# Keys of an attention layer from seven products of halves, laid between the value products, with a gate tensor reloaded per batch

## The chip, the cores and the metric

The kernel runs on one core of a Trainium2 chip. The metric is the device time in microseconds (us) of one execution. Engines are named as in the profile: PE (TensorE: matmul; PEld is its weight load), DVE (VectorE), ACT (ScalarE), POOL (GpSimd), SP (SyncE, which issues the DMAs here). All data are f32.

## The reference, cut to what matters

There are 16 batches of N = 1024 nodes with C = 256 channels. Layer 0 is attention with 4 heads of 64, whose queries come from a gate on an adjacency matrix; layer 1 is a two-stage graph convolution. Each ends in a residual and a layer norm. The part that the change touches:

```python
fea = jnp.transpose(x, (0, 2, 1))
A_s = ...                                  # likeness of the nodes, from channel means
Wg = adj[None, :, :] * A_s
g = jnp.einsum('bcn,bnm->bcm', fea, Wg)
g = jax.nn.relu(g * para.reshape(1, C, N)) # para: the gate tensor
q = jnp.transpose(g, (0, 2, 1)).reshape(B, N, h, hd).transpose(0, 2, 1, 3)
kv = (x @ kv_w).reshape(B, N, 2, h, hd).transpose(2, 0, 3, 1, 4)
k, v = (kv[0], kv[1])                      # keys and values: two halves of one product
attn = jax.nn.softmax(jnp.einsum('bhnd,bhmd->bhnm', q, k) * scale, axis=-1)
out = jnp.einsum('bhnm,bhmd->bhnd', attn, v)
```

The keys of one batch are thus a product of a 256 x 256 half of `kv_w` with the 256 x 1024 transposed input.

## The kernel before, in words

**Order.** Everything is written under a manual schedule: the order in which the program is written is the order of the instructions on each engine. Tiles come from pools; a new tile takes a free slot, and where none is free its first writer waits for the last reader of the old one. The row pool has 23 slots of one 128 x 1024 f32 tile (4 KB in each partition), `row_tile`. PSUM has three tiles of two banks (`big_psum`, or its first bank alone, `half_psum`) and two of one bank (`bank_psum`).

**The loop.** `run` (L834) goes over the batches. For batch b it does attention in four units (`UNITS`: two pairs of heads by two halves of the query nodes). `scores` (L506) computes eight score tiles; ACT takes each one's exponential (L517), and DVE adds them up into `acc` (L521, L523), transposes the sum (L525) and reduces it to `den_part` (L527). `outputs` (L529) multiplies the exponentials with the values and transposes the result on DVE (L538). `add` (L540) folds `den_part` into denominators by a small product on PE (L546), which DVE inverts (L550) and applies.

Between the units lie three gaps (`gap0`, `gap1`, `gap2`) with the graph convolutions of the two batches before: `inner` (L627), `Joined.run` (L796) and `last`. POOL prepares sums for them, `R` (L783 to L786) and, for the queries, `S` (L426 to L429). In `Joined.run` DVE adds a snapshot (L812), which ACT's `relu` (L645) reads; the result is transposed by DVE (L661).

**Queries.** The queries of batch b + 1 come from `FastQueries` (L404): instead of eight products of half matrices it does seven, on sums and differences of the halves, as in Winograd's form of Strassen's method. Its `end` (L469) combines the seven results on DVE (L477 to L484). `scale` (L487) multiplies with `para_sb`, which is on chip from the start, on DVE (L490) and applies a relu on ACT (L491).

**The batch change.** From batch 2's preparation on, the branch `elif more` (L1007 and on) has this order: the last query products, `q.end`, the DMAs for later batches (`load_blocked`, `load_next`), `keys` (L336), `norm.scale` (L325), `norm.spread` (transposes L213, stores L333), `values` (L349). `keys` makes two 128 x 1024 results from eight products of 128 x 128 with 128 x 512 and copies each on ACT (L346). Ahead of the last quarter it calls `between`: `norm.variance`, which folds squares on PE (L244), scales them on DVE (L318) and takes the power -1/2 on POOL (L320), and then `q.scale`. `values` makes four groups of two 128 x 256 blocks, each group in a one-bank PSUM tile, copied by ACT (L358). Then attention of batch b + 1 begins, and it reads `qT`, `kT` and `v`.

**SP's queue.** All loads and stores are issued there, in order. `Queries.load` (L371) issues the adjacency rows of the queries, `load_blocked` (L108) and `load_x` (L96) the inputs.

Of the kernel before, what the change touches and what calls it, by code (L numbers as in the profile page):

```python
# [18 lines left out]
def kernel(  # L19
# [31 lines left out]
    nc = tc.nc  # L51
# [14 lines left out]

    DEN_MIN = 1e-25
    DEN_MAX = 1e28
    ROWS = 23
    S = 32  # L70
    NB = N // S

# [18 lines left out]
    def bank_psum(name):  # L91
        return psum.tile([P, FB], F32, tag="bank", name=name, bufs=2)
# [6 lines left out]
    def row_tile(name):  # L99
        return work.tile([P, N], F32, tag="row", name=name, bufs=ROWS)  # L100

# [16 lines left out]
                          in_=x[0, t0 * P:(t0 + 2) * P, :].rearrange("(t p) c -> p t c", p=P))  # L118
    kvw_sb = const.tile([P, NC, 2 * C], F32, name="kvw_sb")
    nc.scalar.dma_start(out=kvw_sb, in_=kv_w.rearrange("(cc p) f -> p cc f", p=P))  # L120
    para_sb = const.tile([P, NC, N], F32, name="para_sb")
    w1l_sb = const.tile([P, NC, HID], F32, name="w1l_sb")
    w1n_sb = const.tile([P, NC, HID], F32, name="w1n_sb")
    w2l_sb = const.tile([HID, C], F32, name="w2l_sb")
# [1 line left out]
    b1_sb = const.tile([HID, 1], F32, name="b1_sb")  # L126
    b2_sb = const.tile([P, C], F32, name="b2_sb")

    def load_para():
        nc.sync.dma_start(out=para_sb, in_=para.rearrange("o (cc p) a b -> p (o cc) (a b)", p=P))  # L130

    def load_weights():
        nc.sync.dma_start(out=w1l_sb, in_=w1_loop.rearrange("(cc p) f -> p cc f", p=P))
# [67 lines left out]
    def adj_blocked(mt):  # L201
        t = row_tile(f"adjB_{mt}")
        for a in range(Q):
            nc.sync.dma_start(
                out=t[a * S:(a + 1) * S, :].rearrange("k (bn r) -> k bn r", r=S),
                in_=adj[:, mt * P + a * S:mt * P + (a + 1) * S].rearrange("(bn k) r -> k bn r", k=S))
        return t
# [84 lines left out]
    class BlockedNorm:  # L292


        def __init__(self, xB, sums, name):
            self.xB, self.sums, self.name = xB, sums, name
# [39 lines left out]
    def keys(b, xT, between=lambda: None):  # L336
        kT = work.tile([P, NC, N], F32, tag="kT", name=f"kT_{b}")
        for kb in range(NC):
            pk = big_psum(f"k_ps_{b}_{kb}")
            for j in range(NJ):  # L340
                if kb == 1 and j == 1:
                    between()
                for cc in range(NC):
                    nc.tensor.matmul(pk[:, ts(j, FB)], kvw_sb[:, cc, ts(kb, P)], xT[:, cc, ts(j, FB)],  # L344
                                     start=(cc == 0), stop=(cc == NC - 1))
            nc.scalar.copy(kT[:, kb, :], pk)  # L346
        return kT

    def values(b, xT, copy=nc.scalar.copy):  # L349
        v = work.tile([P, NT, C], F32, tag="v", name=f"v_{b}")  # L350
        per = FB // C
        for g in range(NT // per):
            pv = bank_psum(f"v_ps_{b}_{g}")
            for i in range(per):
                for cc in range(NC):
                    nc.tensor.matmul(pv[:, ts(i, C)], xT[:, cc, ts(g * per + i, P)], kvw_sb[:, cc, C:2 * C],  # L356
                                     start=(cc == 0), stop=(cc == NC - 1))
            copy(v[:, g * per:(g + 1) * per, :], pv.rearrange("p (i c) -> p i c", c=C))  # L358
        return v

    class Queries:

# [6 lines left out]
        def load(self, t):  # L369
            self.adj[t] = row_tile(f"adj_{self.b}_{t}")  # L370
            nc.sync.dma_start(out=self.adj[t], in_=adj[t * P:(t + 1) * P, :])  # L371

        def weigh(self, t):

# [22 lines left out]
        def end(self):  # L397
            qT = work.tile([P, NC, N], F32, tag="qT", name=f"qT_{self.b}")
            for cb in range(NC):
                nc.vector.tensor_mul(qT[:, cb, :], self.pg[cb], para_sb[:, cb, :])  # L400
                nc.scalar.activation(qT[:, cb, :], qT[:, cb, :], AF.Relu, scale=QSCALE)  # L401
            return qT

    class FastQueries(Queries):  # L404
# [82 lines left out]

        def scale(self):
            for cb in range(NC):
                nc.vector.tensor_mul(self.qT[:, cb, :], self.qT[:, cb, :], para_sb[:, cb, :])  # L490
                nc.scalar.activation(self.qT[:, cb, :], self.qT[:, cb, :], AF.Relu, scale=QSCALE)  # L491

    class Attention:
# [340 lines left out]
    def run():  # L834
# [11 lines left out]
        q = Queries(0, x_first)  # L846
        for t in range(NT):
            q.load(t)
        load_para()
        blocked = load_blocked(1, "1")  # L850
        tiles = {mt: adj_blocked(mt) for mt in range(3)}
        load_weights()
# [36 lines left out]
        for b in range(B):  # L889
# [57 lines left out]
                q = (FastQueries if c1 else Queries)(b + 1, xb)  # L947
            for u in range(len(UNITS)):
                att.scores(u)
                if u == 3 and between:  # L950
                    for t in (2, TJ + 2, 3, TJ + 3):
                        q.load(t)
                    for t in (2, TJ + 2, 3, TJ + 3):
                        q.likeness(t)
                    q.right(1)
                if u and not between:
                    att.add(u - 1)
                att.outputs(u)
                if u == 2 and more:
                    if c1:  # L960
                        for t in (1, TJ + 1):
                            q.load(t)
                            q.likeness(t)
                            q.times_adj(t)
                    else:
                        for t in range(3):
                            q.load(t)
                            q.weigh(t)
                if u < 3 and between:
                    between[u]()  # L970
                if u == 0 and more and not between:
                    means(q, xb, str(b + 1))()
            norm = BlockedNorm(xB, att.sums, str(b))
            if more and not c1:
                xT = ready["xT"]
                for t in range(3, NT):
                    q.load(t)
                for t in range(3, NT):
                    q.likeness(t)
                tiles[3] = adj_blocked(3)  # L980
                q.times_adj(3)
                q.step(0)
                q.times_adj(4)
                q.step(1)
                att.add(3)
                for mt in range(4, NT):
                    tiles[mt] = adj_blocked(mt)
                q.times_adj(5)
                q.step(2)
                q.step(3)  # L990
                norm.mean()
                q.times_adj(6)
                q.times_adj(7)
                q.step(4)
                norm.squares()
                norm.sum_squares()
                q.step(5)
                q.step(6)
                norm.variance()
                xB = load_blocked(b + 1, f"a{b + 1}")  # L1000
                q.step(7)
                qT = q.end()
                load_next()
                norm.scale()
                norm.spread()
                turn_adj(range(3, NT))
                kT, v = keys(b + 1, xT), values(b + 1, xT)  # L1007
            elif more:
                xT = ready["xT"]
                q.pair(2)  # L1010
                q.step(0)
                q.step(1, lambda: att.add(3))
                q.pair(3)
                q.step(2, lambda: (norm.mean(), norm.squares()))
                q.step(3)
                qT = q.end(norm.sum_squares)
                xB = load_blocked(b + 1, f"a{b + 1}")
                load_next()
                kT = keys(b + 1, xT, lambda: (norm.variance(), q.scale()))
                if not c2:  # L1020
                    adj_sums(rows01, 1)
                norm.scale()
                norm.spread()
                v = values(b + 1, xT)
            else:
                c2.load_h1()
                c2.load_x()
                both.fetch(2, 3)
                c1.inner()
                both.left(nc.gpsimd)  # L1030
                both.fetch(1, 4)
                both.run({1: (lambda: att.add(3),), 2: (norm.mean, norm.squares, norm.sum_squares), 7: (norm.variance,),
                          5: (norm.scale, norm.spread)})
                c1.turn(0)
                c2.last()
                c1.turn(1)
# [33 lines left out]
    with tc.If(count < P):  # L1070
        with tc.For_i(0, B, 1) as b:
            xb = load_x(b, "z")
            xT = channel_major(load_blocked(b, "z"), "xT_z")
            q = Queries("z", xb)
            means(q, xb, "z")()
            kT, v = keys("z", xT), values("z", xT)
            for t in range(NT):
                q.load(t)
                q.weigh(t)
                q.step(t)  # L1080
            safe_attention("z", xb, q.end(), kT, v)
            layernorm(xb, "za")
            conv = GraphConv("z", channel_major(blocked_of(xb, "z"), "x1T_z"), x=xb)
            rows01 = fetch("01", "z")
            conv.inner()
            conv.first(rows01)
            for j in range(NJ):
                conv.turn(j)
            conv.second(rows01)
            conv.last()  # L1090
            conv.moments()
            conv.finish(out[b])
# [29 lines left out]
```

## Time and profile before

Three runs took 2187.68, 2187.73 and 2188.1 us. The profiled execution took 2187.24 us, with a span of 2185.5 us on the core and a granted clock of 0.999.

| engine | busy us | share of the span | instructions |
|---|---|---|---|
| PE | 2168.6 | 99% | 8082 |
| DVE | 1801.7 | 82% | 2347 |
| ACT | 1016.2 | 46% | 1304 |
| POOL | 350.8 | 16% | 192 |

Busy time is the time in which an engine has at least one instruction at work. A row of the groups reads: line, engine, operation, output <- inputs with sizes in partitions x elements, count, then busy time and mean ns of one, then the engine's idle time ahead of them and what ended it. A row of the timeline gives start, length, engine, line, operation, and the count of instructions it joins; an idle time and its releaser stand in brackets. A row of the waits gives who waited for whom, the sum in us, the number of waits and the longest. The batch period in the middle of the run is 134.4 us (first key product at 657.74 us, the next batch's at 792.13 us).

### The profile page before, as it was taken

Reading aid. Unit: us, or ns where it says so; the run is one execution under the profiler, and the core shown is the slowest. Engines: PE = TensorE matmul, PEld = TensorE weight load, DVE = VectorE, ACT = ScalarE, POOL = GpSimd, SP = SyncE. Lnnn points to the kernel's source line nnn. Section 1 sums busy time; section 2 is a strip of 40 time slices with the busy share of each in tenths; the row PEclk is TensorE's granted clock in tenths of the full one; section 3 lists DMA queues with packets and bytes.
Section 4 is the critical chain, followed back from the end, with each engine's and each line's share of the span. In section 5 each row is a group of like instructions: output and inputs, shape, how many; then the busy total and the mean of one; then the engine's idle time right before and its main releaser. Section 6 shows DMA issues by size and latency. Waiting matters only on the chain.

```text
span 2185.5 us, 22862 instructions
## 1 busy us (share of the span) xinstructions
PE 2168.6 (99%) x8082; PEld 1029.9 (47%) x8082; DVE 1801.7 (82%) x2347; ACT 1016.2 (46%) x1304; POOL 350.8 (16%) x192
## 2 busy tenths in 40 slices
PE   9999999999999999999999999999999999999997
PEld 5344444444444444444544445444454444444354
DVE  4978978788898888978889788888888888888965
ACT  4744445544354544445443454444543445534411
POOL 0010120311303112030120302203022130211021
PEclk9999999999999999999999999999999999999999
DMA  9393653736547365563655526556374553743342
GB/s 223 92 121 116 140 149 86 144 118 98 154 107 152 101 94 156 107 161 87 91 170 97 155 87 91 169 97 155 87 105 155 99 153 96 123 138 61 113 138 95
DMA packets 604121, 266.54 MB, mean 122 GB/s; under 512 B 503904, under 2 KB 568288, under 8 KB 604000
## 3 DMA queue, kind: packets, MB, share of 16 engines
q1 hardware_dynamic: 603728, 264.49, 52.7%
q8 instruction: 65, 1.06, 0.2%
q10 hardware_dynamic: 272, 0.52, 0.1%
q14 instruction: 56, 0.46, 0.1%
HBM read 218.76 MB, written 46.20 MB: 121 GB/s over the span
## 4 chain that ended last, share of the span: by engine, by line
PE 69%; DVE 24%; ACT 4%; issue 2%; DMA 0%; DVEq 0%; SPq 0%; POOLq 0%; ACTq 0%; POOL 0%
PE s L514 17%; PE hu_ps L793 17%; PE av L534 16%; DVE acc L523 4%; PE v_ps L356 3%; PE t_ps L632 3%; PE h_ps L700 2%; PE hu_ps L639 2%; PE g_ps L394 2%; PE h_ps L701 2%; DVE wg L386 2%; DVE qT L490 1%; DVE sq_part L313 1%; ACT sq L308 1%; DVE wg L440 1%
## 5 line engine op out<-in xcount | busy, mean ns | idle before, releaser
L517 ACT ACTIVATE pr<-s 128x1024 f32<-128x1024 f32 x512 | 476.1, 1052 | 176.2 <-PE s L514 176.2
L523 DVE TENSOR_TENSOR acc<-acc,pr 128x1024 f32<-128x1024 f32 x384 | 493.4, 1285 | 41.4 <-DVE acc L523 1.4
L514 PE MATMUL s<-qT,kT 64*128 64x512 f32 x2048 | 457.1, 596 | 0.7 <-ACT qT L401 0.7
L534 PE MATMUL av<-pr,v 128*64 128x512 f32 x2048 | 453.6, 595 | 0.0
L514 PEld LDWEIGHTS s<-qT,kT 64*128 64x128 f32 x2048 | 191.2, 186 | 235.9 <-ACT pr L517 112.9
L534 PEld LDWEIGHTS av<-pr,v 128*64 128x64 f32 x2048 | 141.4, 137 | 300.0 <-issue 284.7
L320 POOL TENSOR_TENSOR rstd<-rstd,neg_half 128x32 f32<-128x32 f32 x16 | 100.2, 6260 | 1110.7 <-DVE rstd L318 1110.7
L380 ACT ACTIVATE wg<-c_row,c_col 128x1024 f32<-128x1024 f32 x128 | 147.0, 1149 | 74.2 <-DVE accB L525 55.7
L386 DVE SCALAR_TENSOR_TENSOR wg<-wg,adj 128x1024 f32<-128x1024 f32 x128 | 151.0, 1211 | 22.9 <-ACT wg L381 22.9
L793 PE MATMUL hu_ps<-adj,R 128*128 128x512 f32 x360 | 158.3, 596 | 0.0
L381 ACT ACTIVATE wg<-wg 128x1024 f32<-128x1024 f32 x128 | 135.4, 1058 | 4.1
L308 ACT ACTIVATE sq<-xB_a 128x1024 f32<-128x1024 f32 x32 | 33.8, 1057 | 188.7 <-DVE xB_a L303 187.4
L356 PE MATMUL v_ps<-kvw_sb,xT 128*128 128x256 f32 x512 | 117.0, 382 | 1.5 <-ACT v L358 0.8
L467 PE MATMUL g_ps<-wg,S 128*128 128x512 f32 x224 | 116.7, 603 | 0.0
L344 PE MATMUL k_ps<-xT,kvw_sb 128*128 128x512 f32 x256 | 115.8, 597 | 0.0
L467 PE MATMUL g_ps<-T,S 128*128 128x512 f32 x224 | 114.4, 592 | 0.0
L467 PE MATMUL g_ps<-wg,x 128*128 128x512 f32 x224 | 109.0, 599 | 0.0
L356 PEld LDWEIGHTS v_ps<-kvw_sb,xT 128*128 128x128 f32 x512 | 96.0, 190 | 26.7 <-issue 7.7
L793 PE MATMUL hu_ps<-adjT,t 128*128 128x512 f32 x240 | 105.7, 592 | 0.0
L793 PEld LDWEIGHTS hu_ps<-adj,R 128*128 128x128 f32 x360 | 67.3, 190 | 78.9 <-issue 78.7
L521 DVE TENSOR_TENSOR acc<-pr,pr 128x1024 f32<-128x1024 f32 x64 | 77.5, 1212 | 32.5 <-ACT pr L517 32.4
L325 DVE TENSOR_TENSOR xB_a<-xB_a,rstd 128x1024 f32<-128x1024 f32 x32 | 38.8, 1254 | 60.5 <-POOL rstd L320 60.5
(163 smaller groups left out, 2735.0 us busy)
## 6 DMA issues: line engine op xcount, KB each, us to landing
adj<-in_adj_dram SPq DMA_DIRECT2D x128, 512.0 KB, 4.5
adj<-adjT SPq DMA_DIRECT2D x120, 512.0 KB, 10.2
xB_a<-in_x_dram SPq DMA_DIRECT2D x128, 128.0 KB, 4.0
x1d<-xB_a SPq DMA_DIRECT2D x128, 128.0 KB, 3.4
x<-x1d SPq DMA_DIRECT2D x16, 1024.0 KB, 15.3
xB<-in_x_dram SPq DMA_DIRECT2D x120, 128.0 KB, 4.6
x<-in_x_dram SPq DMA_DIRECT2D x15, 1024.0 KB, 6.8
out_dram<-x SPq DMA_DIRECT2D x15, 1024.0 KB, 4.5
```

The lines of the kernel that those rows point to most:

```text
L320: nc.gpsimd.tensor_tensor(self.rstd, self.rstd, neg_half, ALU.pow)
L344: nc.tensor.matmul(pk[:, ts(j, FB)], kvw_sb[:, cc, ts(kb, P)], xT[:, cc, ts(j, FB)], start=(cc == 0), stop=(cc == NC - 1))
L356: nc.tensor.matmul(pv[:, ts(i, C)], xT[:, cc, ts(g * per + i, P)], kvw_sb[:, cc, C:2 * C], start=(cc == 0), stop=(cc == NC - 1))
L380: nc.scalar.activation(wg, self.c_row, AF.Abs, bias=self.c_col[:, t:t + 1], scale=-1.0)
L381: nc.scalar.activation(wg, wg, AF.Tanh, scale=-0.5)
L386: nc.vector.scalar_tensor_tensor(wg, wg, 1.0, self.adj.pop(t), op0=ALU.add, op1=ALU.mult)
L467: nc.tensor.matmul(self.p[n], x_n[:, k, :], w_n, start=(k == 0), stop=(k == TJ - 1))
L514: nc.tensor.matmul(ps[:, ts(s, FB)], self.kT[rows, pair, ts(mt, P)], self.qT[rows, pair, ts(j, FB)], start=True, stop=True)
L517: nc.scalar.activation(pr, ps, AF.Exp)
L523: nc.vector.tensor_add(acc, acc, pr)
L534: nc.tensor.matmul(pav[s * HD:(s + 1) * HD, :], self.v[:, mt, pair * P + s * HD:pair * P + (s + 1) * HD], self.pr[mt][:, ts(s, FB)], start ...
L793: nc.tensor.matmul(dst, self.x[n][:, k, :], half_adj[w][:, k, :] if w else of_rows(rows, k), start=(start and k == 0), stop=(k == TJ - 1), ...
```

## The change

The keys of batches 2 to 15 come from a new class `KeysValues`; batches 0 and 1 keep `keys` and `values`. `keys` itself is not changed, and `values` is split so that one group can be issued alone (`value_group`).

- The key product is divided into halves: the weights into four blocks of 128 x 128, the input into four of 128 x 512. Seven products of sums and differences replace the eight. The sums of weights are made once, at the start, by POOL, stored to DRAM and loaded per batch (`load`). The sums of the input halves are made per batch by DVE (`sums`), in unit 1 between `scores` and `outputs`.
- `run` issues the seven products with the four value groups between them. Five half results are copied on ACT, two sums are made on DVE and one on POOL. Three products accumulate on results that have been copied in between (`again=True`).
- `norm.variance` and `q.scale` are called at two places of that order, where `keys` called both at one.
- `para_sb` is no longer kept. Each batch loads its two rows (`load_para`), and the row pool has 25 slots in place of 23.

```diff
-    ROWS = 23
+    ROWS = 25
...
-    para_sb = const.tile([P, NC, N], F32, name="para_sb")
...
+    def sum_key_weights():
+        a11, a21, a12, a22 = (kvw_sb[:, cc, ts(kb, P)] for cc in range(NC) for kb in range(NC))
+        t = row_tile("key_sums")
+        s1, s2, s3, s4 = (t[:, ts(n, P)] for n in range(4))
+        nc.gpsimd.tensor_add(s1, a21, a22)
+        nc.gpsimd.tensor_sub(s2, s1, a11)
+        nc.gpsimd.tensor_sub(s3, a11, a21)
+        nc.gpsimd.tensor_sub(s4, a12, s2)
+        nc.sync.dma_start(out=key_sums, in_=t[:, 0:4 * P])
...
+    class KeysValues:
...
+        def sums(self):
+            w11, w12, w21, w22 = (self.xT[:, cc, ts(j, FB)] for cc in range(NC) for j in range(NJ))
+            t13, t24 = (row_tile(f"K_{self.b}_{k}") for k in range(2))
+            t1, t3, t2, t4 = t13[:, 0:FB], t13[:, FB:N], t24[:, 0:FB], t24[:, FB:N]
+            nc.vector.tensor_sub(t1, w12, w11)
+            nc.vector.tensor_sub(t3, w22, w12)
+            nc.vector.tensor_sub(t2, w22, t1)
+            nc.vector.tensor_sub(t4, w21, t2)
+            self.w = {1: w11, 2: w21, 3: w22, 4: t4, 5: t1, 6: t2, 7: t3}
+
+        def load(self):
+            t = row_tile(f"key_sums_{self.b}")
+            nc.sync.dma_start(out=t[:, 0:4 * P], in_=key_sums)
+            a11, a21, a12, a22 = (kvw_sb[:, cc, ts(kb, P)] for cc in range(NC) for kb in range(NC))
+            self.a = {1: a11, 2: a12, 3: t[:, ts(3, P)], 4: a22, 5: t[:, ts(0, P)], 6: t[:, ts(1, P)], 7: t[:, ts(2, P)]}
+
+        def run(self, between, later):
...
+            product(1, first)
+            nc.scalar.copy(p1, first)
+            product(2, third)
+            group(0)
+            product(6, first, again=True)
+            nc.scalar.copy(u1, first)
+            group(1)
+            between()
+            nc.vector.tensor_add(kT[:, 0, 0:FB], p1, third)
+            product(5, first, again=True)
+            nc.scalar.copy(u3, first)
+            product(7, second)
+            nc.scalar.copy(p7, second)
+            group(2)
+            later()
+            product(4, second, again=True)
+            nc.vector.tensor_add(kT[:, 1, 0:FB], u1, second)
+            nc.gpsimd.tensor_add(kT[:, 1, FB:N], u3, p7)
+            product(3, first, again=True)
+            nc.scalar.copy(kT[:, 0, FB:N], first)
+            group(3)
+            return kT, v
...
+        def load_para(self):
+            self.para = []
+            for cb in range(NC):
+                self.para.append(row_tile(f"para_{self.b}_{cb}"))
+                nc.sync.dma_start(out=self.para[cb],
+                                  in_=para[:, cb * P:(cb + 1) * P].rearrange("o p a b -> (o p) (a b)"))
...
         def scale(self):
             for cb in range(NC):
-                nc.vector.tensor_mul(self.qT[:, cb, :], self.qT[:, cb, :], para_sb[:, cb, :])
+                nc.vector.tensor_mul(self.qT[:, cb, :], self.qT[:, cb, :], self.para[cb])
...
-        load_para()
+        sum_key_weights()
+        q.load_para()
...
                 att.scores(u)
+                if u == 1 and between:
+                    kv = KeysValues(b + 1, ready["xT"])
+                    kv.sums()
...
                 q.step(2, lambda: (norm.mean(), norm.squares()))
+                q.load_para()
+                kv.load()
                 q.step(3)
                 qT = q.end(norm.sum_squares)
                 xB = load_blocked(b + 1, f"a{b + 1}")
                 load_next()
-                kT = keys(b + 1, xT, lambda: (norm.variance(), q.scale()))
+                kT, v = kv.run(norm.variance, q.scale)
                 if not c2:
                     adj_sums(rows01, 1)
                 norm.scale()
                 norm.spread()
-                v = values(b + 1, xT)
```

In the changed kernel's `run` the first three PSUM tiles are named `first`, `third` and `second`; `p1`, `u1`, `u3` and `p7` are halves of two row tiles in SBUF.

More of the change, by code (lines that the diff above doesn't have):

```diff
@@ L127 @@
     b2_sb = const.tile([P, C], F32, name="b2_sb")
-    def load_para():
-        nc.sync.dma_start(out=para_sb, in_=para.rearrange("o (cc p) a b -> p (o cc) (a b)", p=P))
+    key_sums = dram.tile([P, 4 * P], F32, tag="key_sums", name="key_sums", bufs=1)
+    def sum_key_weights():
[7 more added lines that the diff above has]
+        nc.sync.dma_start(out=key_sums, in_=t[:, 0:4 * P])
     def load_weights():
@@ L347, in keys, with value_group @@
         return kT
+    def value_group(b, v, xT, g, copy):
+        per = FB // C
+        pv = bank_psum(f"v_ps_{b}_{g}")
+        for i in range(per):
+            for cc in range(NC):
+                nc.tensor.matmul(pv[:, ts(i, C)], xT[:, cc, ts(g * per + i, P)], kvw_sb[:, cc, C:2 * C],
+                                 start=(cc == 0), stop=(cc == NC - 1))
+        copy(v[:, g * per:(g + 1) * per, :], pv.rearrange("p (i c) -> p i c", c=C))
     def values(b, xT, copy=nc.scalar.copy):
         v = work.tile([P, NT, C], F32, tag="v", name=f"v_{b}")
-        per = FB // C
@@ L352, in values @@
[L352 to L358, printed above, removed]
-        return v
+        for g in range(NT * C // FB):
+            value_group(b, v, xT, g, copy)
@@ new lines, in values, with __init__, product, group @@
+        return v
+    class KeysValues:
+        def __init__(self, b, xT):
+            self.b, self.xT = b, xT
+        def sums(self):
[13 more added lines that the diff above has]
+        def run(self, between, later):
+            b, xT = self.b, self.xT
+            kT = work.tile([P, NC, N], F32, tag="kT", name=f"kT_{b}")
+            v = work.tile([P, NT, C], F32, tag="v", name=f"v_{b}")
+            first, third, second = (half_psum(f"k_ps_{b}_{i}") for i in range(3))
+            s12, s34 = (row_tile(f"ksnap_{b}_{k}") for k in range(2))
+            p1, u1, u3, p7 = s12[:, 0:FB], s12[:, FB:N], s34[:, 0:FB], s34[:, FB:N]
+            def product(n, dst, again=False):
+                nc.tensor.matmul(dst, self.a[n], self.w[n], start=not again, stop=True, skip_group_check=again)
+            def group(g):
+                value_group(b, v, xT, g, nc.scalar.copy)
+            product(1, first)
[20 more added lines that the diff above has]
+            return kT, v
@@ L399, in end @@
             for cb in range(NC):
-                nc.vector.tensor_mul(qT[:, cb, :], self.pg[cb], para_sb[:, cb, :])
+                nc.vector.tensor_mul(qT[:, cb, :], self.pg[cb], self.para[cb])
                 nc.scalar.activation(qT[:, cb, :], qT[:, cb, :], AF.Relu, scale=QSCALE)
@@ L1008, in run @@
             elif more:
-                xT = ready["xT"]
                 q.pair(2)
@@ L1014, in run @@
                 q.step(2, lambda: (norm.mean(), norm.squares()))
+                q.load_para()
+                kv.load()
                 q.step(3)
@@ L1080 @@
                 q.step(t)
+            q.load_para()
             safe_attention("z", xb, q.end(), kT, v)
```

## The prediction

> **What bounds the kernel now.** I read the page's first part, then its chain by engine, then the timeline of TensorE (PE), VectorE (DVE) and GpSimd (POOL) around one batch change in the middle (batch 5 to 6, 790 to 846 us), then the waits over one period (657.74 to 792.13 us, from one batch's first key product to the next one's).
>
> ```profile
> PE 2168.6 (99%) x8082; PEld 1029.9 (47%) x8082; DVE 1801.7 (82%) x2347; ACT 1016.2 (46%) x1304; POOL 350.8 (16%) x192
> PE 69%; DVE 24%; ACT 4%; issue 2%; DMA 0%; DVEq 0%; SPq 0%; POOLq 0%; ACTq 0%; POOL 0%
> ...
> L344 PE MATMUL k_ps<-xT,kvw_sb 128*128 128x512 f32 x256 | 115.8, 597 | 0.0
> ```
>
> PE is busy 99% of the span, at full clock in every slice. So PE time taken away is worth its length, if what PE does next isn't then found waiting. DVE (82%) carries a quarter of the chain: it is the engine that could take over. The keys' timeline on PE:
>
> ```profile
> 792.13 5.31 PE L344 MATMUL k_ps<-xT,kvw_sb 128*128 128x512 f32 x12
> 797.28 0.30 PE L244 MATMUL sum_ps<-sq_part,fold 128*128 128x32 f32 x2
> 797.42 1.96 PE L344 MATMUL k_ps<-xT,kvw_sb 128*128 128x512 f32 x4
> 799.22 7.39 PE L356 MATMUL v_ps<-kvw_sb,xT 128*128 128x256 f32 x32
> 806.54 7.14 PE L514 MATMUL s<-qT,kT 64*128 64x512 f32 x32
> ```
>
> One 128x512 f32 product is two records. Twelve records take 797.28 - 792.13 = 5.15, so 0.429 us each and 0.858 a product; the 597 ns of the group overlap. Values take 7.32 us for 32 records; the uninterrupted 128x256 record is half of 0.429, so 6.86. The missing 0.46 is a wait:
>
> ```profile
> PEld v_ps L356 <- ACT v L358: 0.5, 1, 0.5
> DVE rden L550 <- PE den_ps L546: 2.6, 1, 2.6
> DVE snap L812 <- PE hu_ps L793: 2.8, 1, 2.8
> DVE xB_a L325 <- POOL rstd L320: 4.1, 1, 4.1
> ```
>
> A value group waits for its bank, because ACT does a 1.0 us kT copy (L346) and a qT relu first. The other three are DVE's slack: it is idle 4.1 us for POOL's power, 2.6 us for the first unit's denominators, 2.8 us for graph-conv products. What stands behind the first key product until the first add of attention:
>
> ```profile
> 798.09 6.37 POOL L320 TENSOR_TENSOR rstd<-rstd,neg_half 128x32 f32<-128x32 f32 x1 [72.12 <-DVE rstd L318]
> 818.96 1.27 POOL L783 TENSOR_TENSOR R<-h 128x512 f32<-128x512 f32 x1
> 836.21 2.11 POOL L426 TENSOR_TENSOR S<-x 128x512 f32<-128x512 f32 x1 [5.95 <-PE av L534]
> 838.40 2.13 POOL L427 TENSOR_TENSOR S<-S,x 128x512 f32<-128x512 f32 x1
> ...
> 804.50 2.36 DVE L325 TENSOR_TENSOR xB_a<-xB_a,rstd 128x1024 f32<-128x1024 f32 x2 [4.14 <-POOL rstd L320]
> 811.02 7.87 DVE L523 TENSOR_TENSOR acc<-acc,pr 128x1024 f32<-128x1024 f32 x6
> 820.21 1.22 DVE L527 TENSOR_REDUCE den_part<-accB 128x32 f32<-128x1024 f32 x1
> 824.65 0.52 DVE L550 RECIPROCAL rden<-den_ps 64x16 f32<-64x16 f32 x2 [2.60 <-PE den_ps L546]
> 831.98 9.63 DVE L523 TENSOR_TENSOR acc<-acc,pr 128x1024 f32<-128x1024 f32 x6
> ```
>
> See that the same six adds take 7.87 us alone and 9.63 beside two POOL operations, which themselves take 2.11 instead of 1.27: 0.88 us lost per meeting. And den_part ends at 821.43, when PE comes for it (den_ps) at 824.30: 2.87 us of slack.
>
> **What the Trainium skill says.** (1) "SBUF — State Buffer", "Who interferes with whom": a DVE instruction with two SBUF inputs contends with a GpSimd instruction that reads SBUF, the pair being an exclusive lock; one with a single SBUF input doesn't. The 9.63 against 7.87 agrees; that the lock lasts the whole instruction does not fit the power, beside which L490 (two SBUF inputs) runs at its usual 1.249. (2) The same section: DMA never contends with a compute engine. No run here isolates it; PE at full rate through slices of 90% DMA agrees. (3) "GPSIMD Engine Reference", "4.1 Engine selection": two-input elementwise work is about twice as slow on GpSimd; the trace has 1.27 (L783) against 0.69 us (L439). (4) "TensorE: Matmul & The Clock Gate", "Step-by-step: what each phase is for": one matmul's drain overlaps the next one's fill, so the spacing is the price: 429 against 597 ns here.
>
> **The change part by part.** It applies to 14 of 16 batches (2 to 15); batches 0 and 1 keep keys(). The trace of before is the clock.
>
> *PE.* One product fewer: -0.858. With values between, PE's order is P1 792.13, P2 792.99, group 0 793.85, P6 795.6, group 1 796.4, the fold of sq_part 798.15, P5 798.35, P7 799.2, group 2 800.1, P4 801.8, P3 802.7, group 3 803.6, scores 805.3. Each wait, by the nearest row: P2 needs the bank freed by the U add at 792.73; P6 needs the copy of P1 (0.59, as L358), done 793.8; the fold needs sq_part, 795.99, and ACT's copy of group 0, 796.4; P5 the copy of P6, 797.3; P4 the copy of P7, 800.9. All are met. The bank wait of 0.46 goes too, since each group has over 2 us for its bank. Scores need qT's relu and kT's half copy: DVE multiplies by para 799.6 to 802.1, ACT relus 802.5 to 804.6, copies 804.6 to 805.2. That is just in time. Gain 0.858 + 0.46 = **1.3 us a batch** (806.54 to about 805.25).
>
> *ACT.* Five half copies (5 x 0.59 = 2.9) for two whole ones (2.0): +0.9, in idle time (ACT is 46% busy), except as the scores' entry just counted. Zero.
>
> *DVE.* In the tail two kT adds with one SBUF input, 2 x 0.69, inside the 4.1 us wait for the power: zero. In unit 1 the four key sums, 4 x 0.69 = 2.7, behind den_part and ahead of the transpose of o (844.07): they fill the 2.8 us wait for the snap; they can meet S (L428, L429), up to 2 x 0.88 = 1.8 more. Queued behind are o and the snap; an overflow delays ACT's relu by at most 1.8, and DVE waits again 1.9 at h1B (L661) soon after. Between 0 and 0.5; I take 0.
>
> *The power and DVE's chain.* The fold comes 0.9 later (798.15 against 797.28), the rstd at 798.75. Before, the power began beside L490; the fastest of the 16 took 5.44, where no L490 ran at its start. Now it starts beside a kT add with one SBUF input. Taking 5.46 it ends 804.46, no later than before (804.46); taking 6.37, 805.4. At once POOL does the third kT add, 1.27 alone, which meets the scale L325 (two SBUF inputs). A meeting costs DVE between 0.88 (measured above) and 1.27 (the whole POOL operation). Before, the scale begins 804.50, the transposes end 809.14 and DVE waits 0.55; now they end at 810.0 to 810.4 and the adds follow without that wait. They took 9.2 (809.69 to 818.89), so they run to 819.2 or 819.6, and R (L783), which before began at 818.96 just when they were over, now falls inside them: a second 0.88 to 1.27. Transpose and reduction behind them took 2.54, so den_part ends between 822.6 and 823.4. PE arrives at 824.30 - 1.3 = 823.0. **Loss 0 to 0.4; I take 0.2.** With a power of 6.37 it is 0.9 more. Net gain 1.1 a batch, between 0.2 and 1.3.
>
> *DMA and SP's queue.* Per batch two para loads of 512 KB and 256 KB of key sums go out at about 773 to 778, between the adj loads and the xB_a loads (778.37), which they push back by three issues of some 0.7 us (5.80/8). A 512 KB load lands in 4.5 us, so by 783; needed at 795.6 and 799.6. 1.25 MB at the 290 GB/s seen in the busiest stretches is 4.3 us of DMA in a 134 us period at a DMA share of 0.53; behind them x, xB and x1d are used tens of us later. Zero. The row pool has 23 + 2 tiles, the two freed by para_sb; the key sums hold two from unit 1 to the tail and the tail's five are slots released by step 3. Zero; a wait would show on SP's queue.
>
> *Start.* Four POOL operations of 128x128, well under 1.27 each, and a store before para's load at 8.88: POOL is idle there. Under 1 us once; para in batch 1 goes out before xB_a (123.97). Zero.
>
> Sum: 14 x 1.1 = 15.4. Span 2185.5 to 2170.1; this execution was 2187.24, the others 2187.68 to 2188.1, so 2.2 is added to the span: **2172.3 us**.
>
> **The rivals.**
> (A) As summed, 0.75 to 1.35 a batch: 2169 to 2177. For it: 99% PE, all waits met.
> (B) A new wait takes the gain: the power keeps its 6.37 and both meetings cost the whole POOL operation, den_part ends at 824.3, PE stands 1.1 to 1.3 at the first den_ps, gain 0 to 0.2: 2185 to 2188. For it: the 2.87 of slack is eaten by 1.3 (PE early) and up to 0.9 + 1.27 + 1.27, less 0.55 of old idle. Against: the shorter power where L490 is absent.
> (C) Slower, by that mechanism past its point of decision: den_part later than PE by over 1.3 us. One more meeting, L325's second half with a late kT add or an acc add with the tail of R, adds 0.9 to (B), a loss of 0.9 x 14 = 12.6: about 2200. Against: each POOL operation met at most the DVE work of its own length so far.
> (D) A part is lost: the scores' entry has no slack, and ACT's copy or relu misses it by 0.4 to 0.7, or the power alone is long; gain 0.4 to 0.75: 2177 to 2182.
> That the product isn't saved at all is excluded: fewer matmuls are issued and PE has no idle time to hide it.
>
> **How the numbers follow.** A 0.64, D 0.12, B 0.12, C 0.12. About 0.2%, 4.4 us, is what a measurement of this kernel can tell from no change. A and D are faster: 0.76; B 0.12 the same; C 0.12 slower. A's own range is 2167 to 2180; to hold 8 in 10 it reaches into B: 2167 to 2186.
>
> **What would show it.** Right: scores begin about 13.1 us after the first key product (14.41 before), no v_ps wait on ACT; the period is 133.3 in place of 134.4; the power takes 5.4; DVE waits well under 1 us at the first rden. Wrong: PE's load of den_ps waiting for den_part by over 0.5 each batch; scores waiting for ACT's kT copy or relu; acc adds of unit 0 over 9.6 us; SP's queue waiting at para.

## The result, and the profile after

The changed kernel takes 2174.28 us (median of 6 runs, 2172.51 to 2175.69) against 2187.7 us (6 runs, 2187.24 to 2188.1). The ratio is 0.9938, 95% interval 0.9925 to 0.995, a gain of 13.4 us. 2172.3 was predicted, with a range of 2167 to 2186. The profiled execution has a span of 2172.4 us.

The busy times and the chain by engine, from the page:

```profile
PE 2155.6 (99%) x8054; PEld 1026.6 (47%) x8054; DVE 1893.7 (87%) x2431; ACT 1027.7 (47%) x1346; POOL 368.2 (17%) x210
PE 97%; DVE 2%; ACT 0%; DMA 0%; issue 0%; SPq 0%; POOLq 0%; DVEq 0%; POOL 0%
```

PE is still busy 99%, on 28 records less (one product of two records in 14 batches). DVE is 92 us busier, yet its share of the chain fell from 24% to 2%. DVE had been on the chain where its query work ended in ACT's copies and then in the bank wait of the values. That path is gone. The timeline of PE at the change from batch 4 to 5 shows the new order:

```profile
658.55 1.88 PE L408 MATMUL k_ps<-xT,kvw_sb 128*128 128x512 f32 x4
660.26 1.89 PE L363 MATMUL v_ps<-kvw_sb,xT 128*128 128x256 f32 x8
661.99 1.02 PE L408 MATMUL k_ps<-K,key_sums 128*128 128x512 f32 x2
662.85 1.89 PE L363 MATMUL v_ps<-kvw_sb,xT 128*128 128x256 f32 x8
...
669.10 1.02 PE L408 MATMUL k_ps<-xT,key_sums 128*128 128x512 f32 x2
669.96 1.89 PE L363 MATMUL v_ps<-kvw_sb,xT 128*128 128x256 f32 x8
671.78 7.14 PE L596 MATMUL s<-qT,kT 64*128 64x512 f32 x32
```

From the first key product to the scores it is 671.78 - 658.55 = 13.23 us, where it was 14.41. The starts of the first key product of each batch, read the same way along the whole timeline, give this table (us). "Once" is the period from the preparation of batch 2 to that of batch 3, in which DVE also makes adjacency sums (L203 to L206 of the changed kernel); "steady" is the usual one behind it.

| kernel | key product to scores | steady period | "once" |
|---|---|---|---|
| before | 14.41 | 134.38 | 134.21 |
| changed | 13.23 | 133.20 | 137.48 |

So 13 batches gain some 1.18 us each, and one period is 3.27 longer. (One of the 13 entries, in the period that begins at 1457.75, took 13.48; what made it was not found.) DVE and POOL in a steady batch, from their timelines:

```profile
398.79 5.46 POOL L329 TENSOR_TENSOR rstd<-rstd,neg_half 128x32 f32<-128x32 f32 x1 [72.79 <-DVE rstd L327]
404.21 1.28 POOL L430 TENSOR_TENSOR kT<-ksnap 128x512 f32<-128x512 f32 x1
418.93 1.28 POOL L865 TENSOR_TENSOR R<-h 128x512 f32<-128x512 f32 x1 [1.09 <-DMA h<-h1d]
...
399.22 2.35 DVE L572 TENSOR_TENSOR qT<-qT,para 128x1024 f32<-128x1024 f32 x2
404.28 3.43 DVE L334 TENSOR_TENSOR xB_a<-xB_a,rstd 128x1024 f32<-128x1024 f32 x2 [0.69 <-POOL rstd L329]
411.20 7.87 DVE L605 TENSOR_TENSOR acc<-acc,pr 128x1024 f32<-128x1024 f32 x6
423.49 0.52 DVE L632 RECIPROCAL rden<-den_ps 64x16 f32<-64x16 f32 x2 [1.26 <-PE den_ps L628]
```

The power takes 5.46 instead of 6.37. The kT add on POOL meets the scale, which takes 3.43 instead of 2.36 (+1.07). R waits for its input h until 418.93, when the adds are nearly over, so the adds take 7.87 as before. DVE still waits 1.26 for PE at the first denominators, where it waited 2.60: slack is left, and PE doesn't stand.

R does not come at the same time in every batch. In 11 of the 12 steady batches that have an R it waits for h, for 0.2 to 1.2 us. In 8 of these it still meets the last of the adds, but then R is what takes longer (1.63 to 2.15 us in place of 1.27), and the adds keep their 7.87 or 7.88. In one batch h is there in time, R begins earliest, and the adds pay:

```profile
1610.22 8.98 DVE L605 TENSOR_TENSOR acc<-acc,pr 128x1024 f32<-128x1024 f32 x6
1616.85 1.27 POOL L865 TENSOR_TENSOR R<-h 128x512 f32<-128x512 f32 x1
1622.53 0.52 DVE L632 RECIPROCAL rden<-den_ps 64x16 f32<-64x16 f32 x2 [0.17 <-PE den_ps L628]
```

That is 1.11 us more, and of the slack 0.17 is left. PE doesn't stand there either.

In the "once" period it does. First two lines of DVE in the kernel before, then DVE, POOL and PE in the changed kernel:

```profile
262.76 1.22 DVE L194 TENSOR_TENSOR adjT<-adjT,adjT 128x1024 f32<-128x1024 f32 x1
267.42 2.35 DVE L325 TENSOR_TENSOR xB_a<-xB_a,rstd 128x1024 f32<-128x1024 f32 x2
...
265.42 0.69 DVE L429 TENSOR_TENSOR kT<-ksnap,k_ps 128x512 f32<-128x512 f32 x1 [1.33 <-PE k_ps L408]
266.03 1.22 DVE L203 TENSOR_TENSOR adjT<-adjT,adjT 128x1024 f32<-128x1024 f32 x1
267.16 2.29 DVE L204 TENSOR_TENSOR adjT<-adjT,adjT 128x1024 f32<-128x1024 f32 x1
...
271.84 2.35 DVE L334 TENSOR_TENSOR xB_a<-xB_a,rstd 128x1024 f32<-128x1024 f32 x2
...
266.73 1.64 POOL L430 TENSOR_TENSOR kT<-ksnap 128x512 f32<-128x512 f32 x1
...
288.14 0.41 PE L628 MATMUL den_ps<-den_part,fold 128*128 128x32 f32 x2 [2.32 <-DVE den_part L609]
288.48 8.83 PE L596 MATMUL s<-qT,kT 64*128 64x512 f32 x32
```

The busy times in the 9 us behind the stop, of each engine in the same order as on the page, then the granted clock, the DMA share and GB/s:

```profile
288.00:297.00 9.00, 8.86 (x34) 3.92 (x34) 8.78 (x13) 6.14 (x7) 3.10 (x3) 0.81 0.72 96
```

In the kernel before, the four adjacency sums fill the wait for the power, and the scale follows them at 267.42 without idle time. In the changed kernel the sums begin 3.27 later: rstd comes 0.73 later (261.04, before 260.31), the two kT adds ahead of the sums take 1.2, and the second of them waits 1.33 us for product P4. The second sum then takes 2.29 instead of 1.22, beside POOL's kT add. So the scale begins at 271.84, and from there to the end of den_part (286.87 + 1.22 = 288.09) DVE has no idle time. PE stands 2.32 us at den_ps, and then its scores take 8.83 us instead of 7.14, since the granted clock fell to a mean of 0.81.

### The profile page after: what moved, and what is told of

It is laid out like the page before. It is cut to its first block, busy times and chain, and to the rows that moved or that the text cites. A ratio compares the mean times of both kernels' runs of the same rounds, so it can differ in the third digit from the quotient of the medians.

```text
span 2172.4 us, 23124 instructions
## 1 busy us (share of the span) xinstructions
PE 2155.6 (99%) x8054; PEld 1026.6 (47%) x8054; DVE 1893.7 (87%) x2431; ACT 1027.7 (47%) x1346; POOL 368.2 (17%) x210
## 4 chain that ended last, share of the span: by engine, by line
PE 97%; DVE 2%; ACT 0%; DMA 0%; issue 0%; SPq 0%; POOLq 0%; DVEq 0%; POOL 0%
PE s L596 20%; PE av L616 20%; PE hu_ps L875 17%; PE g_ps L549 16%; PE v_ps L363 5%; PE k_ps L408 4%; PE t_ps L714 3%; PE h_ps L782 3%; PE hu_ps L721 2%; PE g_ps L476 2%; PE h_ps L783 2%; DVE acc L605 1%; PE h_ps L736 1%; PE u_ps L765 1%; PE k_ps L353 1%; PE den_ps L628 0%
## 5 line engine op out<-in xcount | busy, mean ns | idle before, releaser
L329 POOL TENSOR_TENSOR rstd<-rstd,neg_half 128x32 f32<-128x32 f32 x16 | 87.1, 5441 | 1108.6 <-DVE rstd L327 1108.6
L607 DVE STREAM_TRANSPOSE accB<-acc 128x1024 f32<-128x1024 f32 x64 | 79.7, 1245 | 3.1
L609 DVE TENSOR_REDUCE den_part<-accB 128x32 f32<-128x1024 f32 x64 | 78.1, 1220 | 2.2
```

What stands on the lines that cost most here:

```text
L329: nc.gpsimd.tensor_tensor(self.rstd, self.rstd, neg_half, ALU.pow)
```

## The experiments

Times are medians; "before" ran beside each on the same chip (2187.40 to 2187.49). Periods are read as above.

**1. The adjacency sums earlier.** Three of the four sums go ahead of the kT add that waits, the fourth behind the keys.

```diff
-        nc.vector.tensor_sub(v[4], w21, v[2])
-        for n in names:
-            nc.sync.dma_start(out=far_adj[n][h], in_=t[n])
+        def rest():
+            nc.vector.tensor_sub(v[4], w21, v[2])
+            for n in names:
+                nc.sync.dma_start(out=far_adj[n][h], in_=t[n])
+        return rest
...
-                kT, v = kv.run(norm.variance, q.scale)
-                if not c2:
-                    adj_sums(rows01, 1)
+                rest = []
+                kT, v = kv.run(norm.variance,
+                               lambda: (q.scale(), None if c2 else rest.append(adj_sums(rows01, 1))))
+                for f in rest:
+                    f()
```

> The changed kernel, with three of the four adjacency sums that DVE makes once, in the change from batch 1 to 2, put ahead of the second kT add (which waits for P4) and the fourth behind it. Theory (the changed kernel loses 2.3 us of PE standing at den_ps in this one batch change, and about 1.9 more because the granted clock drops to 0.81 behind the stop): that period goes from 137.5 to about 133.4 us, the total from 2174.3 to about 2170.2, and no clock below 1.00 behind the first den_ps. Rival (the stop comes from the late landing of x1d and h1, 11.4 and 5.2 us of waits on POOL): period and total stay at 137.5 and 2174.

2170.53 us (2170.49 to 2171.09), ratio 0.9924 (0.991 to 0.9937). The "once" period is 133.58, all others as in the changed kernel. The same lines of DVE and PE:

```profile
267.56 0.68 DVE L433 TENSOR_TENSOR kT<-ksnap,k_ps 128x512 f32<-128x512 f32 x1
...
286.07 0.41 PE L632 MATMUL den_ps<-den_part,fold 128*128 128x32 f32 x2
286.41 7.14 PE L600 MATMUL s<-qT,kT 64*128 64x512 f32 x32
```

And the busy times and clock of the same 9 us:

```profile
288.00:297.00 9.00, 9.00 (x44) 3.35 (x42) 8.72 (x8) 7.02 (x8) 3.69 (x3) 1.00 0.70 192
```

No wait is left in the kT add's line, PE goes through, the scores take 7.14 and the clock is 1.00. The order on DVE made the stop. The late landings shrink in this run too (R waits 2.33 us for h, in the changed kernel 5.17), but they can't have made it: there DVE goes from the sums to den_part without idle time. This is the fastest version. Its runs also lie within 0.6 us of each other, those of the changed kernel within 3.2.

**2. Only the order.** Eight products with value groups between them.

```diff
-                kT = keys(b + 1, xT, lambda: (norm.variance(), q.scale()))
+                kT, v = keys_between_values(b + 1, xT, norm.variance, q.scale)
...
-                v = values(b + 1, xT)
```

> The kernel before, with only the order changed: four value groups between the eight key products, the variance after the second group and the multiplication with para after the third. Theory (of the 1.18 us that a batch gains, 0.86 is the product and 0.32 the bank wait of the values that vanishes): 14 x 0.32 = 4.5, so 2183. Rival (the order is worth nothing, all comes from the product): 2187.7.

2182.42 us, ratio 0.9976 (0.9968 to 0.9985). Key product to scores 14.09, period 134.06 in all batches, also in "once":

```profile
656.84 1.88 PE L369 MATMUL k_ps<-xT,kvw_sb 128*128 128x512 f32 x4
670.93 7.14 PE L539 MATMUL s<-qT,kT 64*128 64x512 f32 x32
```

So the order is worth 14.41 - 14.09 = 0.32. The rest to the changed kernel is 14.09 - 13.23 = 0.86, the length of one product (0.858).

**3. Only the product.** Seven products in a row, then the values.

```diff
             product(1, first)
...
             product(2, third)
-            group(0)
             product(6, first, again=True)
             nc.scalar.copy(u1, first)
-            group(1)
+            product(7, second)
+            nc.scalar.copy(p7, second)
+            product(5, first, again=True)
+            nc.scalar.copy(u3, first)
             between()
...
             product(4, second, again=True)
+            later()
...
-            group(3)
+            for g in range(NT * C // FB):
+                group(g)
```

> The changed kernel with the seven products one after the other (order 1, 2, 6, 7, 5, 4, 3) and all value groups behind them. Theory: the product's 0.86 a batch stays, the bank wait comes back since ACT has two relus and two copies ahead of the first value copy: 14 x 0.86 = 12.0, so 2175.7, with up to 2 us for the stop in the change from batch 1 to 2, 2176 to 2178. Rival (without values between, the products wait for ACT's copies of their own banks): 0.3 to 0.6 a batch more, 2180 to 2186.

2242.33 us, ratio 1.0248 (1.0232 to 1.0264): 68 us slower than the changed kernel. Both theories missed it. The timeline of PE:

```profile
807.48 1.88 PE L408 MATMUL k_ps<-xT,kvw_sb 128*128 128x512 f32 x4
809.20 1.10 PE L408 MATMUL k_ps<-K,key_sums 128*128 128x512 f32 x2
813.30 2.56 PE L408 MATMUL k_ps<-K,key_sums 128*128 128x512 f32 x4 [3.00 <-DVE qT L564]
```

The busy times and, third from the end, the granted clock behind the stop:

```profile
813.30:819.00 5.70, 5.70 (x12) 2.83 (x13) 2.84 (x4) 2.06 (x3) 2.57 (x1) 0.70 0.10 9
```

P7 needs a third two-bank PSUM tile, and DVE still combines the queries from it, with the reductions of the squares in between. PE stands some 3.0 us in every batch (42.0 us in 14 waits) and here then runs at a lower clock: 138.2 a period. So the value groups between do more than save 0.32: they fill the time until that tile is free. The product alone, without a new wait, is known only as the difference of experiment 2 and the changed kernel.

**4, 5 and 6. What accompanies the products.** First all of it (para and key sums loaded, DVE's sums made, 25 row slots) with keys and values as before:

```diff
-                kT, v = kv.run(norm.variance, q.scale)
+                xT = ready["xT"]
+                kT = keys(b + 1, xT, lambda: (norm.variance(), q.scale()))
...
                 norm.spread()
+                v = values(b + 1, xT)
```

> All that comes with the change, without the products: para and key sums loaded per batch, DVE's four key sums made, 25 row slots; keys by eight products and values as before. Theory (loads and sums lie in idle time): 2187.7 within 1 us. Rival (the 1.25 MB a batch or DVE's 2.7 to 4.7 us cost something which the gain hides): 0.2 to 0.5 a batch, 2190 to 2195.

2183.77 us, ratio 0.9983 (0.9976 to 0.999). Neither theory had a gain; key product to scores is 14.20, 0.21 less than before. Two more runs split it: the first without the key sums, the second with them but with para on chip and 23 slots.

```diff
-        sum_key_weights()
...
-                    kv = KeysValues(b + 1, ready["xT"])
-                    kv.sums()
...
-                kv.load()
```

> Of the change only this: para loaded per batch and 25 row slots. No key sums; keys by eight products and values as before. Theory (in the run with loads and sums alone the scores came 0.21 us earlier a batch, because the two more row slots give DVE's last adds of a batch another slot and ACT its likeness rows sooner, and DVE's chain to the relus and copies is that much earlier): 2184 again. Rival (DVE's key sums or the loads of key sums made the difference): 2187.5.

2184.38 us, ratio 0.9985 (0.9978 to 0.9992); 14.22.

```diff
-    ROWS = 25
+    ROWS = 23
...
+    para_sb = const.tile([P, NC, N], F32, name="para_sb")
...
+            self.para = [para_sb[:, cb, :] for cb in range(NC)]
```

> Of the change only the key sums, made by DVE in unit 1 and loaded, both unused; para kept on chip, 23 row slots; keys by eight products and values as before. Theory (row slots make the 0.21 a batch): 2187.5, or slower where a slot is missed. Rival (the sums make it): 2184.

2188.44 us, ratio 1.0005 (0.9996 to 1.0014); 14.41. So the key sums cost nothing in a steady batch, and the gain of 0.2 comes with para's reloading and the two row slots; these two were not separated. The period of the second batch is 119.05 in place of 117.48 here (see experiment 7). In the timeline of ACT the kernel before waits ahead of its likeness rows (wg), the second time for DVE's accB:

```profile
763.37 1.15 ACT L380 ACTIVATE wg<-c_row,c_col 128x1024 f32<-128x1024 f32 x1 [1.30 <-PE av L534]
769.21 1.15 ACT L380 ACTIVATE wg<-c_row,c_col 128x1024 f32<-128x1024 f32 x1 [3.60 <-DVE accB L525]
```

In the run with loads and sums, in the same batch change, it goes on from one row to the next, and waits only once, 0.69 us, ahead of the fourth:

```profile
761.00 1.21 ACT L462 ACTIVATE wg<-c_row,c_col 128x1024 f32<-128x1024 f32 x1
763.20 1.13 ACT L462 ACTIVATE wg<-c_row,c_col 128x1024 f32<-128x1024 f32 x1
```

ACT's relu of the queries and its second kT copy come 0.2 earlier against the first key product (799.20 - 792.13 = 7.07 before, 798.11 - 791.24 = 6.87 here), and with them the bank of the values. That the earlier rows make this is argued, not shown: which slot shifts what was not tried. It is the bank wait that the order removes too: with the seven products the entry is 13.23 with the reloading and without it (experiment 7), so the two gains don't add.

**7. Para on chip in the changed kernel.** 23 slots, seven products, para kept:

```diff
-    ROWS = 25
+    ROWS = 23
...
+    para_sb = const.tile([P, NC, N], F32, name="para_sb")
```

> The changed kernel with para kept on chip from the start, as before, and 23 row slots in place of 25. Theory (two row slots are what the reloading buys, and the key sums need them): waits for row slots appear and the period is longer than 133.2 by 0.2 to 1 us, 2177 to 2188. Rival (23 slots are enough; the reloading is neither needed nor paid for): 2174 within 1 us.

2174.67 us, ratio 0.9942 (0.9925 to 0.9958); steady period 133.20. The rival holds for the steady batch: with the interleaved order the reloading is neither needed nor paid for there. At the start the two slots are missed once: the period of the second batch is 119.10 in place of 117.48, as in experiment 6 (119.05), the other run with key sums and 23 slots. The "once" period is shorter, 135.77 in place of 137.48, though PE stops there too:

```profile
289.59 0.41 PE L627 MATMUL den_ps<-den_part,fold 128*128 128x32 f32 x2 [2.31 <-DVE den_part L608]
289.93 7.14 PE L595 MATMUL s<-qT,kT 64*128 64x512 f32 x32
```

PE stands as long as in the changed kernel, but the scores behind take 7.14, not 8.83, and the granted clock in the 9 us behind the stop (from 289.45 us) is 1.00, not 0.81. So a stop of 2.3 us is not always followed by a lower clock. The stop alone costs this batch 135.77 - 133.20 = 2.6 us; with the lower clock it is 4.3. The four times of this run lie in two pairs, 2173.84 and 2173.94, 2175.40 and 2175.61, and the profiled one is the first. The 1.6 between the pairs would fit a clock that falls in some executions only; no trace shows the others.

**8. The third kT add on DVE.**

```diff
-            nc.gpsimd.tensor_add(kT[:, 1, FB:N], u3, p7)
+            nc.vector.tensor_add(kT[:, 1, FB:N], u3, p7)
```

> The changed kernel with the third kT add on DVE instead of POOL. Theory (the POOL add and the scale meet at DVE's second SBUF input, 1.07 us in the pair of scales, and the slack at den_ps holds it): scale back to 1.18 us each, DVE's wait for den_ps grows by 0.4 to 1, total 2174 within 1 us. Rival (the meeting does cost the end): faster by 0.3 or more a batch, 2170 or less.

2173.40 us (2172.46 to 2174.27), ratio 0.9934 (0.9918 to 0.9951); periods 133.20. The scale and the first denominators on DVE:

```profile
803.38 2.36 DVE L334 TENSOR_TENSOR xB_a<-xB_a,rstd 128x1024 f32<-128x1024 f32 x2
822.61 0.53 DVE L632 RECIPROCAL rden<-den_ps 64x16 f32<-64x16 f32 x2 [2.34 <-PE den_ps L628]
```

The meeting is gone (2.36), and its 1.07 reappear as slack: DVE waits 2.34 where it waited 1.26. The 0.9 us in the median is no gain that can be told: the four times are 2172.46, 2172.79, 2174.02 and 2174.27, and those of the changed kernel lie in the same range (2172.51 to 2175.69). What the profiled executions show is a "once" period of 137.01 in place of 137.48. The second sum doesn't meet the kT add there, and PE stands less long, though its scores are as slow:

```profile
287.42 0.41 PE L628 MATMUL den_ps<-den_part,fold 128*128 128x32 f32 x2 [1.84 <-DVE den_part L609]
287.76 8.83 PE L596 MATMUL s<-qT,kT 64*128 64x512 f32 x32
```

**9. A DVE instruction with two SBUF inputs beside the power's start.**

```diff
-                kT, v = kv.run(norm.variance, q.scale)
+                kT, v = kv.run(lambda: (norm.variance(), q.times_para()), q.scale)
```

`times_para` is the multiplication alone, `scale` then the relu.

> The changed kernel with DVE's two multiplications with para put right behind the rstd, ahead of the first kT add, so that an instruction with two SBUF inputs runs when POOL's power starts. Theory (that instruction holds the power's reads back): the power takes 6.37 in place of 5.44, DVE's slack at den_ps falls from 1.26 to about 0.3, total the same within 1 us. Rival (the power is shorter for another reason): 5.44 again.

2174.71 us, ratio 0.9943 (0.9926 to 0.9959). The list of the power's tile (shortest, median and longest in ns):

```profile
L329 POOL TENSOR_TENSOR rstd<-rstd,neg_half x16: 5438/6352/6370, 134.2 to 2081.5; 128x32 f32<-128x32 f32 x16
```

DVE's timeline, with its waits for the power and for PE:

```profile
538.44 3.42 DVE L334 TENSOR_TENSOR xB_a<-xB_a,rstd 128x1024 f32<-128x1024 f32 x2 [1.58 <-POOL rstd L329]
556.75 0.52 DVE L635 RECIPROCAL rden<-den_ps 64x16 f32<-64x16 f32 x2 [0.38 <-PE den_ps L631]
```

The median is 6352 ns again, and the slack 0.38. So it is what runs on DVE at the power's start that makes 5.44 or 6.35. In the changed kernel the same two multiplications (L572, from 399.22) begin 0.43 us behind the start of the power (398.79) and lie wholly inside it, and it takes 5.46.

**10 and 11. How much slack.** Two, then three, unused transposes of 1.25 us ahead of the scale.

```diff
+                for d in range(2):
+                    nc.vector.transpose(row_tile(f"more_{b}_{d}"), norm.xB[0])
                 norm.scale()
```

> The changed kernel with two transposes of 128x1024 (1.25 us each, their result unused) put on DVE ahead of norm.scale in each batch. Theory (den_part has 1.26 us of slack and no more): 2.5 less the idle 0.69, and R on POOL now falls into the adds, so den_part is about 0.5 late in 13 batches and 2.5 more in the change from batch 1 to 2: 2174.3 + 9 = 2183 if the clock holds, about 2205 if each stop costs 1.7 more by the clock. Rival (the slack is larger, since DVE catches up): 2177.

2177.65 us, ratio 0.9955 (0.9939 to 0.9972). The steady period stays 133.20; all the loss lies in "once", 140.46. The rival holds: the transposes move the scale out of POOL's way (2.36), and DVE still waits 0.63 for PE.

> The same with three transposes. Theory: den_part is about 1.8 late in each batch: 13 x 1.8 + 3.7 = 27, so 2201 if the clock holds, and about 2224 if each stop costs 1.7 more by the clock. Rival (the slack is larger): 2177 to 2185.

2184.74 us, ratio 0.9989 (0.9982 to 0.9995). Here it tips: the steady period is 133.65. PE's line at the first denominators, and the scores behind it:

```profile
829.47 0.41 PE L628 MATMUL den_ps<-den_part,fold 128*128 128x32 f32 x2 [0.19 <-DVE den_part L609]
829.81 7.14 PE L596 MATMUL s<-qT,kT 64*128 64x512 f32 x32
```

The scores begin 31.68 us behind the first key product (798.13), 0.45 later than in the changed kernel, so all of the period's loss arises here, though the trace names 0.19 of it as a wait. Rival (C)'s mechanism is thus real, but its point lies at some 2.5 to 3.7 us of added DVE work, and behind this stop the scores keep 7.14.

## Why the prediction was right, and where its terms were off

- **The bound.** Right: PE's time was what counted, and the product's price was exact (0.858 worked out, 0.86 between experiment 2 and the changed kernel).
- **The bank wait.** The mechanism was right, the size off: 0.46 was put down as all removable, 0.32 came. In the new order 0.09 us is still lost at each of two switches, P7 to group 2 (666.52 - 664.72 = 1.80 for two products) and group 3 to the scores (1.82 for a group that elsewhere takes 1.73). What makes them was not tried.
- **"Loss 0 to 0.4; I take 0.2."** The first meeting took place (1.07, inside the forecast 0.88 to 1.27). The second was priced as a whole one, 0.88 to 1.27, although by the forecast's own times R (818.96) and the adds (to 819.2 or 819.6) overlap by 0.2 to 0.6. It fell on the adds in one of 12 batches only (8.98); in the others R waited for h, and where the two met R paid. The steady loss is zero. The slack at the first denominators is 1.26 to 1.29 in 11 of the 12, where "well under 1 us" was forecast, and 0.17 in the other.
- **"It applies to 14 of 16 batches", all alike.** This step failed. The first of the 14 has the adjacency sums on DVE, with no idle time ahead of the scale, and there "zero" for DVE's kT adds ("inside the 4.1 us wait for the power") was wrong: the wait of the second add stood at the head of DVE's queue, with the sums behind it. It costs 137.48 - 133.20 = 4.3 us, of which experiment 1 recovers 3.9. The trace of before would have shown it: in that batch the sums fill the wait that the forecast counted on.
- **Sum.** The forecast was 14 x 1.1 = 15.4. The steady term gives 14 x 1.18 = 16.5, less the 4.3, 12.2. The rest to 13.1 (spans, 2185.5 to 2172.4) lies outside: two entries of before were 0.35 longer than usual (14.76 in place of 14.41), and the last batch's end came 0.4 sooner; against these stand the one entry of 13.48 and the "once" period of before, which is 0.17 shorter than its steady one. Part of the agreement is luck. In the steady term a bank wait sized 0.14 too large and a loss of 0.2 that didn't come nearly cancel, and the 4.3 fell in one batch only.
- **The power, DMA, SP's queue.** Right: 5.44 came as reasoned (experiment 9), and loads and key sums cost nothing in a steady batch (experiments 4 to 7). Two readings were off without effect. 290 GB/s is not what the busiest stretches show (412 in the 10 us from 970 us of before). And the Trainium skill, "SBUF — State Buffer", "Who interferes with whom", speaks of a lock "for the whole instruction" only for DVE's two-port modes, not for two SBUF inputs, so the power does not go against it.
- **Rivals.** (B) and (D) fell: no wait took the gain, and scores did not wait for ACT. (C) needs two to three more DVE operations (10, 11).
- **Clock.** No step thought of the clock. The Trainium skill, "TensorE: Matmul & The Clock Gate", "What's actually happening", tells that PE's clock has a half-speed state which an idle window of about 3.4 us brings back. The runs agree on the half speed, with a clock of 0.50 in the 2 us from 290 us in the changed kernel. On the length they don't: it came behind a stop of 1.84 us (experiment 8) and one of 2.32, and did not come behind one of 2.31 (experiment 7). What decides stays open.

## What to carry to other kernels

When a change is repeated over iterations, work it out once for the steady one and once for each that carries extra work: here one batch in fourteen took back a quarter of the gain. An instruction that waits is priced by what its engine has queued behind it, so put independent work ahead of it. Fewer matmuls in other PSUM tiles may need a tile that another engine still reads; fill that time with matmuls that don't need it.

## What the runs showed of the hardware that was not expected

- The length of a stop of PE does not tell alone whether the clock falls behind it. Stops of 1.84 us (experiment 8) and 2.32 us (the changed kernel) were followed by a mean clock of 0.81 over 9 us and 1.7 us more for the same scores, and one of 3.0 us by 0.70 over 5.7 us (experiment 3). One of 2.31 us (experiment 7) was followed by full clock. So a stop of about 2.3 us cost 2.6 or 4.3 us.
- A POOL power of 128x32 is lengthened from 5.44 to 6.35 us by DVE instructions with two SBUF inputs at its start, while these keep their 1.2 us each (experiment 9); the same instructions 0.43 us behind its start leave it at 5.46 (the changed kernel). What is held back is the start, not the whole.
- Where POOL's R met DVE's adds, either could be the one that took longer: mostly R (up to 2.15 us in place of 1.27, adds 7.87), once the adds (8.98, R 1.27), in the batch where R began earliest.
